# Keys and queries of an attention kernel from one product, the queries sent through DRAM

## The chip, the cores and the metric

The kernel runs on one NeuronCore of a Trainium2 chip. The metric is device time in microseconds (us), as the median of several runs. Everything is computed in float32.

## The reference, cut to what matters

There are 8 images of 192 channels and 64 x 64 = 4096 positions. Layer 0 is an attention over the positions with 24 channels in query and key; layer 1 is an elementwise chain (a small network of its own for each channel), called the density here.

```python
# layer 0
g = gn(x)                                     # 32 groups, mean 0 and variance 1
q = prelu(conv1x1(g, w1, b1), a1)             # 24 channels
k = prelu(conv1x1(g, w2, b2), a2)             # 24 channels
v = prelu(conv1x1(g, wa, ba), aa)             # 192 channels
score = softmax(einsum('bnc,bcm->bnm', q, k), axis=2)
x = x + einsum('bnm,bmc->bnc', score, v)
# layer 1
g = gn(x)
lower, upper = cumulative(g - 0.5), cumulative(g + 0.5)   # 4 layers 1-3-3-3-1: softplus, tanh
sign = -sign(lower + upper)
x = x + maximum(abs(sigmoid(sign * upper) - sigmoid(sign * lower)), 1e-6)
```

## The kernel before, in words

Channels lie on partitions, three to a row (g of 3), so that 64 partitions hold the 192 channels. The lower 64 partitions hold the first half of the positions and the upper 64 the second half. A **piece** (d, 8 an image) is 256 positions of each half, loaded from x into one of four buffers xi (192 KB for each half); a **chunk** (c, 4 an image) is two pieces.

The stream is a loop of 8 images x 128 **steps**, written out in order by hand. An image has 8 blocks n of 512 query positions, and 16 steps a block. In each step TensorE computes two score products (L769, tile sc) for the next step and two products for a later block's row maxima (L697, tile mx), ScalarE takes the exponential of the scores (L773), and TensorE multiplies the exponentials with the values (L784). VectorE reduces mx to row maxima (L705). The score and maximum products contract over only 24 channels (25 with the maximum's row), so the keys and the queries are kept in all four groups of 32 partitions, and the products of a step use different groups. sc and mx have one PSUM buffer each. The maxima run 22 steps ahead of the scores (LEAD).

What else has to be done goes in between. A scheduler (`job`, `start_job`) starts at most one **job** in a step, which takes a free PSUM bank pair, one of two pairs of scratch tiles (pra, prb), and a few TensorE products; its evaluation on ScalarE and VectorE comes one and two steps later. Jobs are the keys, the queries and the values of a piece, the transposes of the maxima (L734) and of the output (L817), the group norm's averages, and the folding of the norm into the weights (L523 to L555). A keys job is three products over 128 rows (L601), the weights of both halves placed block by block; a queries job is six products over 64 rows, three for each half (L630), whose weights repeat the query channels in the four groups. `prelu` (L583 to L589) evaluates both: two activations with Relu on ScalarE (L585), and one combination on VectorE (L588), whose output is kt for keys and the chunk's tile q for queries.

The keys and values of the next image are made during this one (`prepare`, at steps 30 and later), and its first queries at step 97. The queries of chunk c are made in the 32 steps before their first use (`within`). For each use a piece of x is loaded anew: 28 loads of a piece per image, in kinds of their own ("st" for statistics, "k" and "kv" for keys and values, "q", "v").

The density of image b (L994 to L1026, some 276 VectorE operations of 128 x 1024) is worked off during image b + 1 by credits. In each step VectorE gets a rate that is the work left, divided by the steps left; a job with TensorE time pe and VectorE time cost changes the credit as follows, so that more density work stands beside a longer step:

```python
            credit["DVE"] += pe - cost
            credit["ACT"] += pe - act
...
            rate = left * COST["DVE"] / max(1, (units[0].key[0] + 2) * IMG + 15 - t) + OTHER
```

Some of the density's last part runs on GpSimd. Loads and stores are issued by SyncE in the order of the steps. A head of about 94 us prepares image 0, whose pieces have buffers of their own ("first"), and a tail of about 370 us ends the density of image 7, partly on TensorE (L967).

Of the kernel before, what the change touches and what calls it, by code (L numbers as in the profile page):

```python
# [17 lines left out]
def kernel(  # L18
# [39 lines left out]

    nc = tc.nc
# [26 lines left out]
    small = ctx.enter_context(tc.tile_pool(name="small", bufs=2))  # L86
    dens = ctx.enter_context(tc.tile_pool(name="dens", bufs=1))
# [24 lines left out]
    for i in range(4):  # L112
        t = xin.tile([128, 3, P], F32, tag=f"xi{i}", name=f"xi{i}")
        spare.append(t)
    free = {"xi": 4, "xc": 3}
# [34 lines left out]
    w1r = const.tile([128, 3, 128], F32, name="w1r")  # L150
    w2r = const.tile([128, 3, 128], F32, name="w2r")
    wa_sb = const.tile([128, 3, C], F32, name="wa_sb")
    bq = const.tile([128, 2], F32, name="bq")
    bk = const.tile([128, 2], F32, name="bk")
    ba_row = const.tile([128, C], F32, name="ba_row")
    one_row = const.tile([128, 128], F32, name="one_row")
    slope = const.tile([128, 3], F32, name="slope")
    nslope = const.tile([128, 3], F32, name="nslope")
    for t in (bq, w1r, w2r, ba_row, one_row):
        nc.vector.memset(t, 0.0)  # L160
# [3 lines left out]
    nc.vector.tensor_reduce(out=bk[:, 0:1], in_=ident[:, CR::32], axis=AX.X, op=ALU.add)  # L164
# [11 lines left out]
    for k in range(4):  # L176
        nc.scalar.dma_start(out=bq[32 * k : 32 * k + CR, 0:1], in_=b1.unsqueeze(1))
        nc.scalar.dma_start(out=bk[32 * k : 32 * k + CR, 0:1], in_=b2.unsqueeze(1))
    for i, a in enumerate((a1, a2, aa)):
        nc.scalar.dma_start(out=slope[:, i : i + 1], in_=a.partition_broadcast(128))  # L180

    def spread():

        for k in range(4):
            at = slice(32 * k, 32 * k + CR)
            nc.gpsimd.tensor_copy(w1r[:, :, at], s1)

            p = slice(R * (k % 2), R * (k % 2) + R)
            nc.gpsimd.tensor_copy(w2r[p, :, at], s2[p])
        for g in range(3):  # L190
            nc.gpsimd.tensor_copy(
                wa_sb[:, g, :].rearrange("p (h r) -> p h r", h=3),
                sa[:, g, :].rearrange("p (r h) -> p h r", h=3),
            )
        for s in range(2):
            p = slice(R * s, R * s + 1)
            nc.gpsimd.tensor_copy(
                ba_row[p].rearrange("p (h r) -> p h r", h=3),
                sb[p].rearrange("p (r h) -> p h r", h=3),
            )  # L200

    def negatives():
        for t in (bq, bk):
            nc.vector.tensor_scalar(t[:, 1:2], t[:, 0:1], -1.0, None, ALU.mult)
        nc.vector.tensor_scalar(nslope, slope, -1.0, None, ALU.mult)
# [128 lines left out]
    for k, cols in (("a", F), ("b", 2 * C)):  # L334
        pair = []
        for i in range(2):
            u = work.tile([128, cols], F32, tag=f"pr{k}{i}", name=f"pr{k}{i}")
            pair.append(u)
        scratch.append(pair)
# [58 lines left out]
    def work_off(t, rate):  # L398
        now[0] = t
        run_due(t)  # L400
        start_job(t)
        run_due(t)
        held = set()
        for kind, fn in list(loads):
            if kind == "xi":

                room = free["xi"] - max(0, 2 - sum(k[0] in "qv" for k in xi))
            else:
                room = free["xc" if kind == "xc" else "xi"]
            if room > 0 and kind not in held:  # L410
# [103 lines left out]
    def weights(b, then):  # L514
# [3 lines left out]
        def scale():  # L518
            for k, src, n in (("q", w1r, 2), ("k", w2r, 1), ("v", wa_sb, 1)):
                d = wf[k, b] = fold.tile(  # L520
                    [128, 3, src.shape[2]], F32, tag=f"w{k}", bufs=n, name=f"w{k}_{b}"
                )
                nc.scalar.activation(d, src, AF.Copy, scale=res[:, 1:2])  # L523
            mb = cell["mb"] = fold.tile([128, 128], F32, tag="mb", name=f"mb_{b}")
            nc.vector.tensor_copy(mb, res[:, 0:1].to_broadcast([128, 128]))

        def products():
            pf = cell["pf"]
            p = slice(0, R)
            for g in range(3):  # L530
                cell["write"](nc.tensor.matmul(
                    pf[:, 0:2], lhsT=wf["q", b][p, g, :], rhs=res[p, 0:2],
                    start=g == 0, stop=g == 2,
                ))
            for g in range(3):
                cell["write"](nc.tensor.matmul(
                    pf[:, 2:4], lhsT=wf["k", b][:, g, :], rhs=res[:, 0:2],
                    start=g == 0, stop=g == 2,
                ))
            for g in range(3):  # L540
                cell["write"](nc.tensor.matmul(
                    pf[:, 4 : 4 + C], lhsT=cell["mb"][p], rhs=wf["v", b][p, g, :],
                    start=g == 0, stop=g == 2,
                ))

        def offsets():
            pf = cell["pf"]
            for k, src, at_, n in (("bq", bq, 0, 2), ("bk", bk, 2, 1)):
                d = wf[k, b] = fold.tile([128, 2], F32, tag=k, bufs=n, name=f"{k}_{b}")
                cell["read"](nc.vector.tensor_tensor(  # L550
                    d[:, 0:1], src[:, 0:1], pf[:, at_ : at_ + 1], ALU.subtract
                ))
                nc.vector.tensor_scalar(d[:, 1:2], d[:, 0:1], -1.0, None, ALU.mult)
# [38 lines left out]

    def keys(b, d, what, done):
        t = xi[what, b, d]

        def make(pk, u):
# [3 lines left out]
            for g in range(3):  # L600
                write(nc.tensor.matmul(  # L601
                    pk[:, 0:P], lhsT=wf["k", b][:, g, :], rhs=t[:, g, :],
# [3 lines left out]
            c, h = divmod(d, 2)  # L606
            p = slice(64 * (c % 2), 64 * (c % 2) + 64)
            at_ = (c // 2) * F + h * P
            first, last = prelu(
                ("k", b, d), kt[b][p, at_ : at_ + P], pk[p, 0:P], wf["bk", b][p], nslope[p, 1:2],  # L610
                [x[p, 0:P] for x in u], read,
            )
            return [
                (0, lambda: None, 0.0, 0.0, 1.3), (1, first, 0.0, 0.9, 0.0),
                (2, last, 0.45, 0.0, 0.0),
# [4 lines left out]
    def queries(b, d, what, done):  # L620
        t = xi[what, b, d]
        c, h = divmod(d, 2)

        def make(pq, u):
            if (b, c) not in qt:
                qt[b, c] = work.tile([128, 2, F], F32, tag="q", bufs=2, name=f"q_{b}_{c}")
            for g in range(3):
                for s in range(2):
                    p = slice(R * s, R * s + R)
                    nc.tensor.matmul(  # L630
                        pq[:, s, 0:P], lhsT=wf["q", b][p, g, :], rhs=t[p, g, :],
                        start=g == 0, stop=g == 2,
                    )
            done()
            first, last = prelu(
                ("q", b, d), qt[b, c][:, :, h * P : h * P + P], pq[:, :, 0:P], wf["bq", b], nslope[:, 0:1],
                [x[:, 0:F].rearrange("p (s n) -> p s n", s=2) for x in u],
            )
            return [
                (0, lambda: None, 0.0, 0.0, 1.4), (1, first, 0.0, 1.4, 0.0),  # L640
                (2, last, 0.75, 0.0, 0.0),
            ]

        job(make, h, 0.5 if d == 2 else 2, 2, F)
# [46 lines left out]
    def max_products(b, n, j, k, sc):  # L691
        assert all(i in made for i in (("q", b, n), ("k", b, 2 * k), ("k", b, 2 * k + 1)))
# [539 lines left out]
    def use(b, d, what, t, k, q, v, after=0):  # L1232

        left = [k + q + 2 * v]
# [6 lines left out]
        def begin():  # L1241
            if what != "first":
                visit(b, d, what)
            at(max(now[0] + 4, after), work)

        def work():
            if q:
                queries(b, d, what, done)
# [6 lines left out]
        if what == "first":  # L1255
            at(t, work)
        else:
            at(t, lambda: request("q" if what in "qv" else "xi", begin))

    def prepare(b, t):  # L1260
# [7 lines left out]
        def normed():  # L1268
            for i, c in enumerate(ORDER):
                for h in range(2):  # L1270
                    what = "kv" if i < 2 else "k"
                    use(b, 2 * c + h, what, max(now[0], t + 30 + 6 * (2 * i + h)), 1, 0, i < 2)

            for h in range(2):
                use(b, h, "q", t + 92, 0, 1, 0, t + 97)
# [4 lines left out]
        for i in (2, 3):  # L1280
            for h in range(2):
                use(b, 2 * ORDER[i] + h, "v", t + 100 + 4 * i + 2 * h, 0, 0, 1, t + 107 + 4 * i)
        for h in range(2):
            use(b, 2 + h, "q", t + 122, 0, 1, 0, t + IMG)

    def within(b, t):
        for d in range(4 if b else 2, NP):
            at_ = t + 32 * (d // 2 - 1)
            use(b, d, "q" if b else "first", at_ - 6 if b else at_, 0, 1, 0, at_)
# [31 lines left out]
    todo = [(queries, 0), (keys, 0), (queries, 1)] + [(keys, d) for d in range(1, NP)]  # L1321
# [6 lines left out]
    while todo or ahead:  # L1328
# [10 lines left out]
        if (0, 3, 3) in [i for _, i in pair]:  # L1339
            max_end(0, 0)  # L1340
        go_on()
# [72 lines left out]
```

## Time and profile before

| | |
|---|---|
| median of 3 runs | 4918.28 us (4916.8 to 4919.44) |
| time of the profiled execution | 4916.79 us |
| its span | 4915.0 us |
| mean granted TensorE clock | 0.987 |
| first scores / last step's scores start | 94.05 / 4545.37 us |

The span runs from the first to the last instruction of the profiled execution; its time has 1.8 us more around it. In a group row of the profile, the columns after "x" and the count are the busy time of the whole group in us and the mean of one instruction in ns, then the engine's idle time before these instructions, with what ended it. A float32 product shows as two MATMUL rows.

### The profile page before, as it was taken

To read this page: it belongs to the slowest core of one execution; us is meant where nothing else is said; L and a number is where in the kernel's file an instruction comes from. 1 tells how busy PE (TensorE), PEld (TensorE's weight loads), DVE (VectorE), ACT (ScalarE), POOL (GpSimd) and SP (SyncE) were. 2 spreads that over 40 slices of the span, in tenths; PEclk is the share of its full clock that TensorE was granted. 3 is DMA by queue.
4 is the path that set the end of the run, shared out by engine and by line. 5 is a ranking of instruction groups with operands and counts; after the bars stand their busy time and mean duration, and the time that the engine had idled before them with its cause. 6 is when DMAs were issued, how large, how long until landed. Compare 5 with 4: busy or idle time off the path is not lost.

```text
span 4915.0 us, 69887 instructions
## 1 busy us (share of the span) xinstructions
PE 4740.1 (96%) x29152; PEld 3505.3 (71%) x29152; DVE 4312.6 (88%) x4442; ACT 3194.5 (65%) x3709; POOL 514.0 (10%) x506
## 2 busy tenths in 40 slices
PE   7999999999999999999999999999999999999496
PEld 5777777777777777777777777777777777777232
DVE  5433359999999999999999999999999999998987
ACT  2333347776767766776776767776767767676765
POOL 0000001111011110210111200111111111111000
PEclk9999999999999999999999999999999999999798
DMA  2000020111200111010110111011111101000000
GB/s 56 26 22 18 14 52 4 32 28 31 51 18 18 42 37 34 23 37 24 42 30 21 32 40 40 18 31 32 31 34 32 28 22 28 11 22 5 9 13 13
DMA packets 111953, 135.49 MB, mean 28 GB/s; under 512 B 14738, under 2 KB 93076, under 8 KB 111636
## 3 DMA queue, kind: packets, MB, share of 16 engines
q1 hardware_dynamic: 110432, 130.65, 10.9%
q8 instruction: 228, 3.74, 0.3%
q14 instruction: 89, 0.73, 0.1%
q10 hardware_dynamic: 1204, 0.37, 0.0%
HBM read 105.82 MB, written 25.17 MB: 27 GB/s over the span
## 4 chain that ended last, share of the span: by engine, by line
PE 78%; DVE 16%; ACT 4%; issue 1%; POOL 1%; DMA 0%; ACTq 0%; SPq 0%; DVEq 0%; POOLq 0%
PE b L784 46%; PE sc L769 18%; DVE d L1026 10%; DVE rm L705 4%; PE b L658 4%; PE b L967 2%; PE b L630 2%; PE b L601 1%; PE sc_tail L967 1%; PE mx_tail L967 1%; PE mx L697 1%; PE b L817 1%; ACT d L1019 1%; ACT d L1009 1%; ACT e L773 1%
## 5 line engine op out<-in xcount | busy, mean ns | idle before, releaser
L784 PEld LDWEIGHTS b<-v,e 128*128 128x128 f32 x16384 | 2655.1, 190 | 777.0 <-issue 772.5
L784 PE MATMUL b<-v,e 128*128 128x193 f32 x16384 | 2958.9, 334 | 0.0
L773 ACT ACTIVATE e<-sc 128x1024 f32<-128x1024 f32 x1024 | 1046.7, 1022 | 1456.3 <-PE mx L697 1414.0
L705 DVE TENSOR_REDUCE rm<-mx 128x1 f32<-128x1024 f32 x1002 | 1223.3, 1221 | 459.6 <-PE mx L697 454.2
L769 PE MATMUL sc<-q,k 25*128 25x512 f32 x4096 | 1155.2, 640 | 16.8 <-ACT e L773 16.4
L697 PE MATMUL mx<-k,q 24*128 24x512 f32 x4008 | 1130.4, 640 | 4.9 <-DVE rm L705 4.9
L1026 DVE SCALAR_TENSOR_TENSOR d<-d,wsp,d 128x1024 f32<-128x1024 f32 x768 | 988.0, 1288 | 44.3 <-ACT d L1019 33.6
L1026 DVE SCALAR_TENSOR_TENSOR d<-d,lc,d 128x1024 f32<-128x1024 f32 x765 | 981.6, 1291 | 18.1 <-ACT d L1003 5.1
L1026 DVE SCALAR_TENSOR_TENSOR d<-d,tf,d 128x1024 f32<-128x1024 f32 x543 | 683.9, 1280 | 3.5 <-ACT d L1009 3.4
L1009 ACT ACTIVATE d<-d 128x1024 f32<-128x1024 f32 x543 | 569.6, 1055 | 57.1 <-DVE d L1026 55.7
L769 PEld LDWEIGHTS sc<-q,k 25*128 25x128 f32 x4096 | 306.2, 182 | 250.2 <-issue 195.8
L1114 POOL MEMSET pause<- 128x1 f32 x240 | 23.7, 99 | 3965.9 <-DVE d L1026 3965.9
L1019 ACT ACTIVATE d<-d,cb,wsp 128x1024 f32<-128x1024 f32 x351 | 433.3, 1235 | 0.8 <-DVE d L1026 0.2
L994 ACT ACTIVATE d<-xc,bn,wn 128x1024 f32<-128x1024 f32 x288 | 354.1, 1236 | 2.8 <-DVE bn L491 2.0
L1003 ACT ACTIVATE d<-xc,bn,wn 128x1024 f32<-128x1024 f32 x255 | 315.7, 1238 | 0.0
L697 PEld LDWEIGHTS mx<-k,q 24*128 24x128 f32 x4008 | 299.6, 182 | 16.9 <-DVE rm L705 13.5
L1149 POOL TENSOR_TENSOR d<-d,d 128x512 f32<-128x512 f32 x80 | 169.5, 2119 | 0.2
L1161 POOL TENSOR_TENSOR d<-d,d 128x512 f32<-128x512 f32 x80 | 167.7, 2097 | 0.0
L1169 POOL TENSOR_TENSOR d<-d,d 128x512 f32<-128x512 f32 x80 | 156.4, 1955 | 2.3 <-POOL pause L1114 0.6
L658 PE MATMUL b<-wv,xi 64*128 64x192 f32 x1344 | 139.5, 340 | 1.4 <-ACT pra L585 1.4
L658 PEld LDWEIGHTS b<-wv,xi 64*128 64x128 f32 x1344 | 106.5, 186 | 26.9 <-issue 20.9
L967 PE MATMUL b<-d,v 128*128 128x512 f32 x204 | 95.2, 618 | 17.0 <-ACT d L994 17.0
(171 smaller groups left out, 2373.5 us busy)
## 6 DMA issues: line engine op xcount, KB each, us to landing
xi<-in_x_dram SPq DMA_DIRECT2D x392, 192.0 KB, 3.4
xc<-in_x_dram SPq DMA_DIRECT2D x64, 384.0 KB, 8.0
out_dram<-xc SPq DMA_DIRECT2D x96, 256.0 KB, 3.2
d<-in_x_dram SPq DMA_DIRECT2D x16, 192.0 KB, 4.0
d<-in_wat_dram ACTq DMA_DIRECT2D x2, 144.0 KB
cb<-in_den_b_dram SPq DMA_DIRECT2D x6, 2.2 KB, 2.1
ff<-in_den_f_dram SPq DMA_DIRECT2D x6, 2.2 KB, 2.2
bq<-in_b_dram ACTq DMA_DIRECT2D x4, 0.1 KB
```

Of the source, the lines that this page charges most:

```text
L658: nc.tensor.matmul(pv[:, s, 0:C], lhsT=t[p, g, k * 128 : k * 128 + 128] if g < 3 else one_row[p], rhs=wf["v", b][p, g, :] if g < 3 else wf ...
L697: nc.tensor.matmul(sc[:, s, :], lhsT=tile_of(qt[b, n // 2], n, j)[r], rhs=kt[b][r, u : u + F], start=True, stop=True,)
L705: nc.vector.tensor_reduce(out=rowmax[b, n][:, j, k : k + 1], in_=sc, axis=AX.XY, op=ALU.max)
L769: nc.tensor.matmul(sc[:, s, :], lhsT=kt[b][r, k : k + 128], rhs=qt[b, n // 2][r, :, u : u + 256], start=True, stop=True,)
L773: return lambda: nc.scalar.activation(e, sc, AF.Exp)
L784: nc.tensor.matmul(a[:, j, 0 : C + 1], lhsT=e[:, s, j * 128 : j * 128 + 128], rhs=v[:, s, p % 4, :], start=p == 0 and s == 0 and j % 2 == ...
L967: nc.tensor.matmul(out[:, h, :], lhsT=diag[g][:, 3 * i + n - 1 if n else 9 + i, :], rhs=src[:, h * F : h * F + F], start=n == 0, stop=n == 3,)
L994: nc.scalar.activation(self.buf[k], self.src(), AF.Tanh, bias=bn[:, s, g, 0, i : i + 1], scale=wn[:, g, 0, i : i + 1],)
L1003: nc.scalar.activation(self.buf[k], self.src(), AF.Identity, bias=bn[:, s, g, 1, i : i + 1], scale=wn[:, g, 1, i : i + 1],)
L1009: nc.scalar.activation(self.buf[k], self.buf["l", k[1], k[2]], AF.Tanh)
L1019: nc.scalar.activation(self.buf[k], self.buf["l", n - 1, 0], AF.Identity, bias=offset, scale=wsp[:, g, w : w + 1],)
L1026: nc.vector.scalar_tensor_tensor(dst, src, factor, dst, ALU.mult, ALU.add)
```

## The change

The weights of keys and queries are placed side by side in two tiles `wr`, one for the even and one for the odd chunks. Three products over 128 rows now give both, keys in one half of the 128 output partitions and queries in the other. One evaluation writes them into a tile `kq` of 128 x 256 (three buffers). From there two DMAs of SyncE bring the keys into kt and the queries into a DRAM tile `qd`. `queries(b, c)` then loads a chunk's queries from DRAM four times, once into each group of 32 partitions. There are three buffers xi instead of four, the loads of x for queries are gone, all loads of pieces stand in one line, and both pairs of scratch tiles are 384 columns wide.

```diff
-    for i in range(4):
+    for i in range(3):
         t = xin.tile([128, 3, P], F32, tag=f"xi{i}", name=f"xi{i}")
         spare.append(t)
-    free = {"xi": 4, "xc": 3}
+    free = {"xi": 3, "xc": 3}
...
-        for k in range(4):
-            at = slice(32 * k, 32 * k + CR)
-            nc.gpsimd.tensor_copy(w1r[:, :, at], s1)
-
-            p = slice(R * (k % 2), R * (k % 2) + R)
-            nc.gpsimd.tensor_copy(w2r[p, :, at], s2[p])
+        for i in range(2):
+            for k in range(4):
+                at = slice(32 * k, 32 * k + CR)
+                p = slice(R * (k % 2), R * (k % 2) + R)
+                nc.gpsimd.tensor_copy(wr[i][p, :, at], (s2 if k // 2 == i else s1)[p])
...
-    for k, cols in (("a", F), ("b", 2 * C)):
+    for k in "ab":
         pair = []
         for i in range(2):
-            u = work.tile([128, cols], F32, tag=f"pr{k}{i}", name=f"pr{k}{i}")
+            u = work.tile([128, 2 * C], F32, tag=f"pr{k}{i}", name=f"pr{k}{i}")
...
+    qd = []
+    for i in range(2):
+        t = dram.tile([NC, 64, F], F32, tag=f"qd{i}", name=f"qd{i}")
+        qd.append(t)
+
     def keys(b, d, what, done):
         t = xi[what, b, d]
+        c, h = divmod(d, 2)
+        i = c % 2
...
                 write(nc.tensor.matmul(
-                    pk[:, 0:P], lhsT=wf["k", b][:, g, :], rhs=t[:, g, :],
+                    pk[:, 0:P], lhsT=wf[i, b][:, g, :], rhs=t[:, g, :],
                     start=g == 0, stop=g == 2,
                 ))
             done()
-            c, h = divmod(d, 2)
-            p = slice(64 * (c % 2), 64 * (c % 2) + 64)
-            at_ = (c // 2) * F + h * P
+            kq = work.tile([128, P], F32, tag="kq", bufs=3, name=f"kq_{b}_{d}")
             first, last = prelu(
-                ("k", b, d), kt[b][p, at_ : at_ + P], pk[p, 0:P], wf["bk", b][p], nslope[p, 1:2],
-                [x[p, 0:P] for x in u], read,
+                None, kq, pk[:, 0:P], wf["b", i, b], nslope[:, i : i + 1],
+                [x[:, 0:P] for x in u], read,
             )
+
+            def move():
+                last()
+                k, q = (slice(64 * j, 64 * j + 64) for j in (i, 1 - i))
+                u = (c // 2) * F + h * P
+                nc.sync.dma_start(out=kt[b][k, u : u + P], in_=kq[k])
+                nc.sync.dma_start(out=qd[b % 2][c, :, h * P : h * P + P], in_=kq[q])
+                at(now[0] + 1, lambda: made.update((("k", b, d), ("qd", b, d))))
+
             return [
                 (0, lambda: None, 0.0, 0.0, 1.3), (1, first, 0.0, 0.9, 0.0),
-                (2, last, 0.45, 0.0, 0.0),
+                (2, move, 0.45, 0.0, 0.0),
             ]
...
-    def queries(b, d, what, done):
-        t = xi[what, b, d]
-        c, h = divmod(d, 2)
-        def make(pq, u):
-            if (b, c) not in qt:
-                qt[b, c] = work.tile([128, 2, F], F32, tag="q", bufs=2, name=f"q_{b}_{c}")
-            for g in range(3):
-                for s in range(2):
-                    p = slice(R * s, R * s + R)
-                    nc.tensor.matmul(
-                        pq[:, s, 0:P], lhsT=wf["q", b][p, g, :], rhs=t[p, g, :],
-                        start=g == 0, stop=g == 2,
-                    )
...
-        job(make, h, 0.5 if d == 2 else 2, 2, F)
+    def queries(b, c):
+        assert all(("qd", b, 2 * c + h) in made for h in range(2))
+        q = qt[b, c] = work.tile([128, 2, F], F32, tag="q", bufs=2, name=f"q_{b}_{c}")
+        for k in range(4):
+            nc.sync.dma_start(
+                out=q[32 * k : 32 * k + 32],
+                in_=qd[b % 2][c].rearrange("(s r) n -> r s n", s=2),
+            )
+        made.add(("q", b, c))
...
-            for h in range(2):
-                use(b, h, "q", t + 92, 0, 1, 0, t + 97)
+            at(t + 97, lambda: queries(b, 0))
...
-        for h in range(2):
-            use(b, 2 + h, "q", t + 122, 0, 1, 0, t + IMG)
...
-        for d in range(4 if b else 2, NP):
-            at_ = t + 32 * (d // 2 - 1)
-            use(b, d, "q" if b else "first", at_ - 6 if b else at_, 0, 1, 0, at_)
+        for c in range(1, NC):
+            at(t + 32 * (c - 1) + 1, lambda c=c: queries(b, c))
...
-    todo = [(queries, 0), (keys, 0), (queries, 1)] + [(keys, d) for d in range(1, NP)]
+    todo = [(keys, d) for d in range(NP)]
...
+        if ("qd", 0, 1) in made and (0, 0) not in qt:
+            queries(0, 0)
```

More of the change, by code (lines that the diff above doesn't have):

```diff
@@ L86 @@
     small = ctx.enter_context(tc.tile_pool(name="small", bufs=2))
+    dram = ctx.enter_context(
+        tc.tile_pool(name="dram", bufs=1, space=bass.MemoryType.DRAM)
+    )
     dens = ctx.enter_context(tc.tile_pool(name="dens", bufs=1))
@@ L148 @@
             nc.vector.tensor_copy(gq[:, s, :, i], gs)
-    w1r = const.tile([128, 3, 128], F32, name="w1r")
-    w2r = const.tile([128, 3, 128], F32, name="w2r")
+    wr = []
+    bb = []
+    slope = []
+    for i in range(2):
+        w = const.tile([128, 3, 128], F32, name=f"wr{i}")
+        wr.append(w)
+        w = const.tile([128, 1], F32, name=f"bb{i}")
+        bb.append(w)
+        w = const.tile([128, 1], F32, name=f"slope{i}")
+        slope.append(w)
     wa_sb = const.tile([128, 3, C], F32, name="wa_sb")
-    bq = const.tile([128, 2], F32, name="bq")
-    bk = const.tile([128, 2], F32, name="bk")
     ba_row = const.tile([128, C], F32, name="ba_row")
     one_row = const.tile([128, 128], F32, name="one_row")
-    slope = const.tile([128, 3], F32, name="slope")
+    vslope = const.tile([128, 1], F32, name="vslope")
     nslope = const.tile([128, 3], F32, name="nslope")
-    for t in (bq, w1r, w2r, ba_row, one_row):
+    for t in (*wr, ba_row, one_row):
         nc.vector.memset(t, 0.0)
@@ L162 @@
     nc.vector.memset(one_row[R : R + 1], 1.0)
-    nc.vector.tensor_reduce(out=bk[:, 0:1], in_=ident[:, CR::32], axis=AX.X, op=ALU.add)
+    for i in range(2):
+        nc.vector.tensor_reduce(
+            out=bb[i], in_=ident[:, 64 * i + CR : 64 * i + 64 : 32], axis=AX.X, op=ALU.add
+        )
     st = bufs[0]
@@ L175 @@
         nc.scalar.dma_start(out=sb[R * s : R * s + 1], in_=ba.unsqueeze(0))
-    for k in range(4):
[L177 to L180, printed above, removed]
-    def spread():
-        for k in range(4):
-            at = slice(32 * k, 32 * k + CR)
-            nc.gpsimd.tensor_copy(w1r[:, :, at], s1)
-            p = slice(R * (k % 2), R * (k % 2) + R)
-            nc.gpsimd.tensor_copy(w2r[p, :, at], s2[p])
+    for i in range(2):
+        for k in range(4):
+            b_ = b2 if k // 2 == i else b1
+            nc.scalar.dma_start(out=bb[i][32 * k : 32 * k + CR], in_=b_.unsqueeze(1))
+        for k in range(2):
+            a = a2 if k == i else a1
+            nc.scalar.dma_start(
+                out=slope[i][64 * k : 64 * k + 64], in_=a.partition_broadcast(64)
+            )
+    nc.scalar.dma_start(out=vslope, in_=aa.partition_broadcast(128))
+    def spread():
+        for i in range(2):
+            for k in range(4):
+                at = slice(32 * k, 32 * k + CR)
+                p = slice(R * (k % 2), R * (k % 2) + R)
+                nc.gpsimd.tensor_copy(wr[i][p, :, at], (s2 if k // 2 == i else s1)[p])
         for g in range(3):
@@ L202, in negatives @@
     def negatives():
-        for t in (bq, bk):
-            nc.vector.tensor_scalar(t[:, 1:2], t[:, 0:1], -1.0, None, ALU.mult)
-        nc.vector.tensor_scalar(nslope, slope, -1.0, None, ALU.mult)
+        for i, a in enumerate((*slope, vslope)):
+            nc.vector.tensor_scalar(nslope[:, i : i + 1], a, -1.0, None, ALU.mult)
     negmax = const.tile([128, 4, 128], F32, name="negmax")
@@ L404, in work_off @@
         for kind, fn in list(loads):
[L405 to L410, printed above, removed]
+            if free[kind] > 0 and kind not in held:
                 loads.remove((kind, fn))
@@ L518, in scale @@
         def scale():
-            for k, src, n in (("q", w1r, 2), ("k", w2r, 1), ("v", wa_sb, 1)):
+            for k, src in ((0, wr[0]), (1, wr[1]), ("v", wa_sb)):
                 d = wf[k, b] = fold.tile(
-                    [128, 3, src.shape[2]], F32, tag=f"w{k}", bufs=n, name=f"w{k}_{b}"
+                    [128, 3, src.shape[2]], F32, tag=f"w{k}", name=f"w{k}_{b}"
                 )
@@ L529, in products @@
             p = slice(0, R)
-            for g in range(3):
-                cell["write"](nc.tensor.matmul(
-                    pf[:, 0:2], lhsT=wf["q", b][p, g, :], rhs=res[p, 0:2],
-                    start=g == 0, stop=g == 2,
[L534 to L539, printed above, removed]
+            for i in range(2):
+                for g in range(3):
+                    cell["write"](nc.tensor.matmul(
+                        pf[:, 2 * i : 2 * i + 2], lhsT=wf[i, b][:, g, :], rhs=res[:, 0:2],
+                        start=g == 0, stop=g == 2,
+                    ))
             for g in range(3):
@@ L547, in offsets @@
             pf = cell["pf"]
-            for k, src, at_, n in (("bq", bq, 0, 2), ("bk", bk, 2, 1)):
-                d = wf[k, b] = fold.tile([128, 2], F32, tag=k, bufs=n, name=f"{k}_{b}")
+            for i in range(2):
+                d = wf["b", i, b] = fold.tile([128, 2], F32, tag=f"b{i}", name=f"b{i}_{b}")
                 cell["read"](nc.vector.tensor_tensor(
-                    d[:, 0:1], src[:, 0:1], pf[:, at_ : at_ + 1], ALU.subtract
+                    d[:, 0:1], bb[i], pf[:, 2 * i : 2 * i + 1], ALU.subtract
                 ))
@@ L591, in prelu @@
         return first, last
+    qd = []
+    for i in range(2):
+        t = dram.tile([NC, 64, F], F32, tag=f"qd{i}", name=f"qd{i}")
+        qd.append(t)
     def keys(b, d, what, done):
         t = xi[what, b, d]
+        c, h = divmod(d, 2)
+        i = c % 2
         def make(pk, u):
@@ L616, in make @@
             ]
         job(make, d % 2, cols=P)
-    def queries(b, d, what, done):
-        t = xi[what, b, d]
-        c, h = divmod(d, 2)
-        def make(pq, u):
-            if (b, c) not in qt:
-                qt[b, c] = work.tile([128, 2, F], F32, tag="q", bufs=2, name=f"q_{b}_{c}")
-            for g in range(3):
-                for s in range(2):
-                    p = slice(R * s, R * s + R)
-                    nc.tensor.matmul(
-                        pq[:, s, 0:P], lhsT=wf["q", b][p, g, :], rhs=t[p, g, :],
-                        start=g == 0, stop=g == 2,
-                    )
[L634 to L637, printed above, removed]
-            )
[L639 to L642, printed above, removed]
-        job(make, h, 0.5 if d == 2 else 2, 2, F)
+    def queries(b, c):
+        assert all(("qd", b, 2 * c + h) in made for h in range(2))
+        q = qt[b, c] = work.tile([128, 2, F], F32, tag="q", bufs=2, name=f"q_{b}_{c}")
+        for k in range(4):
+            nc.sync.dma_start(
+                out=q[32 * k : 32 * k + 32],
+                in_=qd[b % 2][c].rearrange("(s r) n -> r s n", s=2),
+            )
+        made.add(("q", b, c))
@@ L691, in max_products @@
     def max_products(b, n, j, k, sc):
-        assert all(i in made for i in (("q", b, n), ("k", b, 2 * k), ("k", b, 2 * k + 1)))
+        assert all(i in made for i in (("q", b, n // 2), ("k", b, 2 * k), ("k", b, 2 * k + 1)))
         for s in range(2):
@@ L1230, in look, with use @@
         at(t, lambda: request("xi", begin))
-    def use(b, d, what, t, k, q, v, after=0):
-        left = [k + q + 2 * v]
+    def use(b, d, what, t, k, v, after=0):
+        left = [k + 2 * v]
         def done():
@@ L1241, in begin @@
         def begin():
-            if what != "first":
-                visit(b, d, what)
+            visit(b, d, what)
             at(max(now[0] + 4, after), work)
         def work():
-            if q:
-                queries(b, d, what, done)
             if k:
@@ L1253, in work @@
                     values(b, d, i, what, done)
[L1255 to L1258, printed above, removed]
+        at(t, lambda: request("xi", begin))
     def prepare(b, t):
@@ L1271, in normed @@
                     what = "kv" if i < 2 else "k"
-                    use(b, 2 * c + h, what, max(now[0], t + 30 + 6 * (2 * i + h)), 1, 0, i < 2)
-            for h in range(2):
-                use(b, h, "q", t + 92, 0, 1, 0, t + 97)
+                    use(b, 2 * c + h, what, max(now[0], t + 30 + 6 * (2 * i + h)), 1, i < 2)
+            at(t + 97, lambda: queries(b, 0))
         for d in range(NP):
@@ L1281, in prepare @@
             for h in range(2):
-                use(b, 2 * ORDER[i] + h, "v", t + 100 + 4 * i + 2 * h, 0, 0, 1, t + 107 + 4 * i)
-        for h in range(2):
-            use(b, 2 + h, "q", t + 122, 0, 1, 0, t + IMG)
+                use(b, 2 * ORDER[i] + h, "v", t + 100 + 4 * i + 2 * h, 0, 1, t + 107 + 4 * i)
     def within(b, t):
-        for d in range(4 if b else 2, NP):
-            at_ = t + 32 * (d // 2 - 1)
-            use(b, d, "q" if b else "first", at_ - 6 if b else at_, 0, 1, 0, at_)
+        for c in range(1, NC):
+            at(t + 32 * (c - 1) + 1, lambda c=c: queries(b, c))
         for c in range(2):
```

## The prediction

> **What bounds the kernel now.** I read the page's busy times and chain first, then the chain and the busy times of single 16-step stretches, then the timeline for the length of one step, and last the groups that the change touches.
>
> ```profile
> span 4915.0 us, 69887 instructions
> PE 4740.1 (96%) x29152; PEld 3505.3 (71%) x29152; DVE 4312.6 (88%) x4442; ACT 3194.5 (65%) x3709; POOL 514.0 (10%) x506
> ...
> PE 78%; DVE 16%; ACT 4%; issue 1%; POOL 1%; DMA 0%; ACTq 0%; SPq 0%; DVEq 0%; POOLq 0%
> ```
>
> The chain runs on TensorE for 78% of the span and on VectorE for 16%; no DMA is in it. The mean hides the middle, so here are the busy times of two stretches of one image (length; PE, PEld, DVE, ACT, POOL; granted clock, DMA share, GB/s), and the chain of the first by line:
>
> ```profile
> 2057.63:2129.41 71.78, 71.78 (x463) 54.39 (x462) 69.86 (x68) 51.94 (x61) 8.76 (x8) 1.00 0.09 25
> 2129.41:2195.65 66.24, 66.12 (x407) 49.95 (x406) 65.08 (x62) 50.70 (x57) 13.76 (x12) 1.00 0.24 50
> ...
> by line: PE b L784 47.2%; PE sc L769 18.9%; DVE d L1026 15.7%; DVE rm L705 6.4%; PE b L658 4.2%; PE b L630 4.2%; PE b L817 0.9%; DVE q L740 0.8%; DVE v L588 0.7%; DVE k L588 0.7%; PE mx L697 0.6%; issue 0.2%
> ```
>
> TensorE is busy without a gap, VectorE 97 to 98%. The query products (L630) stand in the chain with 4.2% of 71.78 us = 3.0 us, the whole of the two that run there. The timeline gives their price: from one step's scores to the next,
>
> ```profile
> 1428.76 0.70 PE L769 MATMUL sc<-q,k 25*128 25x512 f32 x2
> ...
> 1432.64 0.70 PE L769 MATMUL sc<-q,k 25*128 25x512 f32 x2
> ...
> 2092.34 0.70 PE L769 MATMUL sc<-q,k 25*128 25x512 f32 x2
> ...
> 2096.22 1.57 PE L630 MATMUL b<-xi,wq 64*128 64x256 f32 x12
> 2097.71 0.70 PE L769 MATMUL sc<-q,k 25*128 25x512 f32 x2
> ```
>
> A step without a job takes 3.88 us, one with a query job 2097.71 - 2092.34 = 5.37. Read so over the whole stream, steps with a key job take 5.18 and with a value job 5.38, almost all at these same lengths: TensorE sets the step. Scores run from 94.05 to 4545.37; image 0 takes 555 us, images 1 to 6 take 560 to 566.
>
> ```profile
> L630 PE MATMUL b<-xi,wq 64*128 64x256 f32 x672 | 87.7, 393 | 0.0
> L601 PE MATMUL b<-xi,wk 128*128 128x256 f32 x336 | 81.8, 379 | 0.1
> L585 ACT ACTIVATE pra<-b,bq 128x512 f32<-128x512 f32 x126 | 79.4, 686 | 0.7 <-PE b L630 0.7
> L588 DVE SCALAR_TENSOR_TENSOR q<-pra,nslope,pra 128x512 f32<-128x512 f32 x64 | 52.6, 822 | 4.5 <-ACT pra L585 4.5
> L588 DVE SCALAR_TENSOR_TENSOR k<-prb,nslope,prb 64x256 f32<-64x256 f32 x47 | 23.4, 498 | 2.5 <-ACT prb L585 2.1
> ```
>
> **The change part by part.** *Query jobs go.* Sixty-two run in the stream (six for image 0, eight for each of the seven others) and two before it. Each costs 5.37 - 3.88 = 1.50 us of TensorE, all of it on the path: 62 x 1.50 = 93 us. ScalarE loses two activations of 686 ns a job and VectorE one operation of 0.74 us (the median of L588's q); these ran beside TensorE and shorten nothing by themselves.
>
> *The joint product.* The key product already streams 256 columns through 128 rows with 128 weight columns, of which 64 are then thrown away. The new weights have the same shape, so a key step stays at 5.18 us. Its two activations and its VectorE operation go from 64 to 128 partitions of 256 elements. No row has that form; rows of 128 x 384 and 128 x 512 cost ScalarE 490 and 686 ns against 462 for 64 x 256, so time follows the elements of a partition: between zero (same columns) and, if it doubled, 0.9 us on ScalarE and 0.5 on VectorE. I take zero. The folded weights and offsets of an image (L523 to L555) keep their number; a product of 64 rows (264 ns) becomes one of 128 (267 ns).
>
> *The round trip.* A piece gets two moves of 64 KB (keys into kt, queries to DRAM), a chunk four loads of 128 KB: 32 DMAs an image, against 16 loads of x of 192 KB that go; 3.1 MB against 3.1 MB. SyncE takes 1.18 us for two issues, so 32 take 19 us of 560, against 9 that go. A move waits on SyncE for the piece's VectorE operation, and later loads of x and stores of the output stand behind it. It stands in its own step, though, and x is loaded four steps (15.5 us) ahead of its use. VectorE has to find one of three kq buffers free, so it waits for moves three pieces back, at least two steps ago. The trace has no such DMA; the nearest row is the load of x:
>
> ```profile
> xi<-in_x_dram SPq DMA_DIRECT2D x392, 192.0 KB, 3.4
> ```
>
> Four issues (2.4 us) and 3.4 us to landing make some 6 us; the loads are issued nine steps, at least 35 us, ahead of the first maximum product that reads them, and the queries have been written some 50 steps earlier. Beside that row a rule of the Trainium skill speaks against the change: "DMA: Bandwidth & Descriptors", section "Anatomy of one DMA", gives each transfer about 2 us that do not shrink with its size, and its section "Bandwidth" wants transfers of 1 MiB and calls those under 64 KB dominated by descriptors. By its fit (given for GpSimd's path, so an estimate here) 64 and 128 KB take 2.15 and 2.3 us, 16 of each 71 us an image; were these paid in line, the kernel would lose 570 us and the sum would turn over. By the trace DMA has 0% of the chain although a 192 KB load takes 3.4 us, because it starts steps ahead. I take zero for the stream and keep a few us a chunk as the upper end. If the 35 us of cover were gone, each chunk would cost its 6 us, 31 x 6 = 186 us.
>
> *Three x buffers for four.* Twenty pieces an image are loaded instead of 28, and the scheduler hands out a buffer only after the product that frees it. Zero; at most a job comes some steps later.
>
> *The density's order.* Query jobs gave VectorE slack: 1.50 - 0.74 = 0.76 us each. The scheduler credits VectorE 1.4 us and charges 0.75 for each; without it the same density work is spread evenly, 8 x 0.65 = 5.2 us an image over 128 steps, also into stretches that are at 98 to 99% already. An image of VectorE work goes from 547.5 us (the sum of eight stretches) to 541.5, TensorE's image from about 563 to 551: VectorE would be at 98.3% instead of 97.2%. The maximum product (L697) has one PSUM buffer, so a late reduction (L705) stops TensorE. Stretches that are at 99% today are at most 1.4 us longer than TensorE needs, most under 0.5. With half a us more in most of eight stretches I give back 3 us an image for images 1 to 6, and 5 of the 9 us of the last image, where the chain is more VectorE than TensorE: 18 + 5 = 23.
>
> *The head.* First products now need queries that have been to DRAM: keys of piece 1 are evaluated at about 40 us, two moves issue to 41.2, land at 43.5; four loads to 46, landing near 49, and the move of piece 3 stands behind them on SyncE. The first maximum product starts at 46.9 now, so 2 us are lost. Two fewer jobs shorten the end of the head by two value-only rounds of 1.4 us. Net -1, between -4 and +4. The tail after 4546 us is untouched: zero.
>
> Sum against the profiled execution's 4916.8 us: -93 + 23 - 1 = -71, so 4846. The median of the runs shown is 1.5 us above it, so 4847.
>
> **Rivals.** *VectorE becomes the bound.* For it: the 16% in the chain, 97 to 98% busy, the single buffer of mx. Then images 1 to 7 gain only what VectorE loses, 0.74 us for each of the 54 query jobs in their steps, 40 us, while image 0, with no density beside it, keeps its 8 x 1.5 = 12: 52 us in all, 4866. Against it: 10 us of VectorE an image stay idle at the new length. *No give-back.* The 99% stretches show that the schedule can be that tight: 93 + 3, 4822. *Late queries.* Here the kernel gets slower: L697 waits at the first step of each chunk for the loads, with everything behind it on TensorE. It takes over when the loads land 71/31 = 2.3 us past the 35 us, that is, when SyncE's queue is held for some 30 us. For it: SyncE is in order and has waits of up to 119.6 us (for a product that frees an x buffer). Against it: those are waits in program order, which end at the step in which the load stands. At 5 us late a chunk: 4846 + 155 = 5001. *The joint product is not free*: with key evaluation doubled, 64 x 0.5 us on a full VectorE, 32 us come back, 4879; if waits for kq buffers cost VectorE another 39/64 = 0.6 us a piece, no change remains.
>
> **How the numbers follow.** Likeliest 0.53 (4834 to 4858 on its own); VectorE-bound 0.22 (4858 to 4875); no give-back 0.14 (4818 to 4834); costs that eat it all, within 0.2%, 0.04; late queries 0.07. The range 4827 to 4872 leaves out late queries, the tie and the ends of two cases. 0.2% is about 10 us, what a measurement of this kernel can tell from no change: faster 0.89, same 0.04, slower 0.07.
>
> **What would show it.** Right: no L630-like group; key steps still 5.18 us; empty steps mostly at 3.88 with some longer ones, VectorE over 98% in the middle; image 0 at about 543 us and images 1 to 6 at 553 to 555; no row in which PE waits for a DMA after the head. Wrong: PE mx waiting for q's load; kq operations of VectorE waiting for DMA; key steps above 5.3; images above 558.

## The result, and the profile after

The changed kernel takes 4848.81 us (median of 4 runs, 4845.56 to 4850.88) against 4918.86 before (the three runs of the table ahead of the prediction and a fourth): a ratio of 0.9858, 95% interval 0.9844 to 0.9872. It is 70 us faster; 71 were forecast for the profiled executions. The page of its profiled execution (4845.56 us, the fastest of its four):

```profile
span 4843.8 us, 68352 instructions
PE 4656.6 (96%) x28384; PEld 3443.8 (71%) x28384; DVE 4260.6 (88%) x4378; ACT 3116.6 (64%) x3581; POOL 523.3 (11%) x506
...
PE 79%; DVE 14%; ACT 4%; issue 1%; POOL 1%; DMA 0%; ACTq 0%; DVEq 0%; POOLq 0%
...
xi<-in_x_dram SPq DMA_DIRECT2D x280, 192.0 KB, 3.4
...
q<-qd SPq DMA_DIRECT2D x128, 128.0 KB, 2.6
k<-kq SPq DMA_DIRECT2D x64, 64.0 KB, 1.9
qd<-kq SPq DMA_DIRECT2D x64, 64.0 KB, 2.1
```

TensorE has 84 us less to do. The new transfers land in 1.9 to 2.6 us, and DMA still has 0% of the chain. The groups of the changed lines, by form (after the bar: busy us of the group, mean ns of one, then idle time before):

```profile
L620 PE MATMUL b<-xi,w 128*128 128x256 f32 x336 | 81.7, 379 | 0.0
...
L596 ACT ACTIVATE prb<-b,b 128x256 f32<-128x256 f32 x100 | 41.6, 472 | 0.5 <-PE b L620 0.5
...
L599 DVE SCALAR_TENSOR_TENSOR kq<-prb,nslope,prb 128x256 f32<-128x256 f32 x53 | 25.2, 476 | 4.0 <-ACT prb L596 4.0
```

The joint product costs what the key product did (81.8 us, 379 ns), and twice the partitions cost its evaluation next to nothing (462 and 498 ns before). No group like the query products is left.

Read from the start of each step's scores, image by image:

| part | before, us | after, us | difference | forecast |
|---|---|---|---|---|
| head (to the first scores) | 94.05 | 88.88 | -5.2 | -1 |
| image 0 | 555.3 | 543.1 | -12.2 | -12 |
| images 1 to 6 together | 3380.4 | 3329.8 | -50.6 | -54 |
| image 7 to its last step | 515.6 | 511.3 | -4.3 | -4 |
| tail | 369.6 | 370.8 | +1.2 | 0 |
| span | 4915.0 | 4843.8 | -71.2 | -71 |

Images 1 to 6 gain 8.4 us each instead of 12. Where the rest went is seen when the steps of an image are set against the shortest step with the same job (3.88 us for none, 5.18 keys, 5.38 values and so on). What lies above that in images 2 to 6, in us an image (a step is counted by the start of its scores):

| steps | before | after |
|---|---|---|
| 0 to 12 | 0.0 | 0.0 to 0.1 |
| 13 to 17 | 3.1 to 4.8 | 9.3 to 11.4 |
| 18 to 33 | 1.2 to 2.9 | 1.1 to 2.9 |
| 34 to 127 | 2.3 to 4.9 | 0.6 to 3.2 |

The growth is in one place, and most of it in one step: of the 9.3 to 11.4 us step 17 has 5.5 to 7.2 (1.9 to 3.6 before). These are the steps 16 and 17 of image 4 in the timeline of the changed kernel (start, duration in us, engine, line), and then two stretches of it with the granted TensorE clock in the third column from the right:

```profile
2361.96 3.66 DVE L1037 SCALAR_TENSOR_TENSOR d<-d,tf,d 128x1024 f32<-128x1024 f32 x3
...
2365.53 2.67 DVE L1037 SCALAR_TENSOR_TENSOR d<-d,lc,d 128x1024 f32<-128x1024 f32 x2
...
2368.12 1.22 DVE L716 TENSOR_REDUCE rm<-mx 128x1 f32<-128x1024 f32 x1
```

```profile
2361.63 1.13 PE L708 MATMUL mx<-k,q 24*128 24x512 f32 x4
...
2365.50 1.13 PE L780 MATMUL sc<-q,k 25*128 25x512 f32 x4
2369.39 1.77 PE L708 MATMUL mx<-k,q 24*128 24x512 f32 x4 [2.77 <-DVE rm L716]
2371.09 5.51 PE L795 MATMUL b<-v,e 128*128 128x193 f32 x16
2376.53 0.70 PE L780 MATMUL sc<-q,k 25*128 25x512 f32 x2
```

```profile
2365.50:2371.00 5.50, 2.73 (x9) 0.59 (x8) 5.39 (x7) 2.26 (x4) 0.00 (x0) 0.89 0.01 3
2371.00:2376.53 5.53, 5.53 (x18) 5.01 (x16) 4.84 (x5) 1.05 (x1) 0.00 (x0) 0.50 0.00 0
```

VectorE does five density operations before the reduction at 2368.12, which is due when the maximum products that start at 2361.63 are done. TensorE can't start the next maximum product, because mx has one buffer, and stands for 2.77 us. Then the value products take 5.51 us instead of 2.88: the granted clock is 0.50 through the rest of the step. A step of 3.88 us lasts 11.03.

The same stall stands in step 17 of all five images, but the slow clock after it has two lengths. Here is the whole step, first of image 4 and then of image 5:

```profile
2365.50:2376.53 11.03, 8.26 (x25) 5.60 (x24) 10.23 (x11) 3.31 (x4) 0.00 (x0) 0.69 0.00 1
2921.58:2930.99 9.41, 6.64 (x26) 4.47 (x25) 9.27 (x11) 3.31 (x4) 0.00 (x0) 0.82 0.00 1
```

A mean clock of 0.69 over 11.03 us is half clock for 6.8 us, and 0.82 over 9.41 us is half clock for 3.4. Images 2 and 6 are like image 5 (9.40 and 9.44 us), image 3 is like image 4 (10.96). The difference of 1.6 us is the price of 3.4 us at half clock. By that estimate the slow clock has 3.3 of the 7.15 us in images 3 and 4 and 1.7 of the 5.5 us in the others, and the stall, with the products that no longer overlap, has 3.8 in each.

The schedule itself, as the code works it out, says why so much density work stands there. An image's density is due by step 15 of the image after the next, and the rate is the work left divided by the steps left. If the work is late, the rate runs away:

```
rate (us a step) and, in brackets, density operations placed, steps 10 to 14, images 2 to 6
before   3.0-3.3 (2-3)   3.15 (2)   3.35 (2)   3.76 (2)   4.98 (3)
after    3.3-3.5 (2-3)   3.46 (2)   3.76 (1)   4.98 (3)   6.20 (5)
```

### The profile page after: what moved, and what is told of

Same layout as the page of the kernel before. It is cut to its first block, busy times and chain, and to the rows that moved or that the text cites. A ratio compares the mean times of both kernels' runs of the same rounds, so it can differ in the third digit from the quotient of the medians.

```text
span 4843.8 us, 68352 instructions
## 1 busy us (share of the span) xinstructions
PE 4656.6 (96%) x28384; PEld 3443.8 (71%) x28384; DVE 4260.6 (88%) x4378; ACT 3116.6 (64%) x3581; POOL 523.3 (11%) x506
## 4 chain that ended last, share of the span: by engine, by line
PE 79%; DVE 14%; ACT 4%; issue 1%; POOL 1%; DMA 0%; ACTq 0%; DVEq 0%; POOLq 0%
PE b L795 48%; PE sc L780 18%; DVE d L1037 9%; PE b L669 4%; DVE rm L716 3%; PE b L978 2%; PE b L620 1%; PE sc_tail L978 1%; PE mx_tail L978 1%; PE b L828 1%; ACT e L784 1%; PE mx L708 1%; ACT d L1005 1%; ACT d L1030 1%; ACT d L1020 1%
## 5 line engine op out<-in xcount | busy, mean ns | idle before, releaser
L1005 ACT ACTIVATE d<-xc,bn,wn 128x1024 f32<-128x1024 f32 x288 | 353.6, 1234 | 12.2 <-DVE bn L506 11.4
```

The lines of the kernel that those rows point to most:

```text
L1005: nc.scalar.activation(self.buf[k], self.src(), AF.Tanh, bias=bn[:, s, g, 0, i : i + 1], scale=wn[:, g, 0, i : i + 1],)
```

## The experiments

**Only TensorE's part back.** The old jobs' six products, 62 times, on constant operands; 62 jobs, no evaluation.

```diff
+            for g in range(3):
+                for s in range(2):
+                    p = slice(R * s, R * s + R)
+                    nc.tensor.matmul(
+                        pq[:, s, 0:P], lhsT=wr[0][p, g, :], rhs=kt[b][p, 0:P],
+                        start=g == 0, stop=g == 2,
+                    )
+            return [(0, lambda: None, 0.0, 0.0, 1.4)]
```

> The changed kernel with the old query jobs' six products put back as jobs (62 of them, at their old steps, with constant weights and keys as data, their result unused; no evaluation, no load of x). Theory A, that TensorE's time is what was gained and VectorE's lateness in a few steps gives some of it back: 62 x 1.50 = 93 us come back, less the some 25 us of give-back, since VectorE gets its slack again: 4905 to 4920 us, image 0 back at 555, steps with such a job 5.38. Theory B, that VectorE was and is the bound and the gain came from its fewer operations: less than 45 us come back, below 4893. Theory C, that the gain came from fewer loads and a shorter head: under 20 us.

Measured: 4915.48 us (12 runs), a ratio of 0.9996 to before, 95% interval 0.9988 to 1.0005. Image 0 takes 555.1 us again and images 2 to 6 563 to 564; the steps with such a job take 5.38. The returned products, as the trace has them:

```profile
L663 PE MATMUL b<-k,wr x744: 376/376/480, 109.5 to 4322.0; 64*128 64x256 f32 x186
```

They are the old ones to the nanosecond (376 in the middle). With TensorE's time back the whole gain is gone, so fewer loads and fewer VectorE operations are worth nothing while the products are there. (The jobs bring back their places in the scheduler and their 1.4 us of credit as well; that the products themselves are the time is read from the steps of 5.38 us.) The 67 us that came back are less than 93 mainly because steps 13 to 17 got calmer again (5.5 to 7.0 us for 9.3 to 11.4). They are not as calm as before the change: this schedule, too, reaches a rate of 6.20 at step 14 and puts four or five operations there. In images 2 to 6 TensorE then stands for some 3.7 us once, in step 15, and waits for an exponential, which stands behind density operations on ScalarE (read in image 4).

**Only VectorE's part back.** One operation of the old size at each old place; the scheduler is not told.

```diff
+            at(t0 + 2, lambda: ghost2(b))
...
+        nc.vector.scalar_tensor_tensor(gu[0], kt[b][:, 0:F], nslope[:, 0:1], kt[b][:, 0:F], ALU.mult, ALU.add)
```

> The changed kernel with one more VectorE operation of 128 x 512 for each old query job in the stream (62, at the steps of the old ones; it combines a tile of keys, its output is unused; nothing else moves, the scheduler is not told). Theory A: VectorE at 98% has little room, so images 1 to 7 lose part of 54 x 0.74 = 40 us, image 0 nothing: 10 to 30 us, 4859 to 4879. Theory B (VectorE is the bound everywhere): the full 40 us or more, 4889 and up. Theory D (TensorE alone is the bound): within 5 us of the changed kernel.

Measured: 4867.7 us, 19 more than the changed kernel (ratio to before 0.9899, 0.9883 to 0.9916). The tile's rows:

```profile
L664 DVE SCALAR_TENSOR_TENSOR gu<-k,nslope x62: 734/742/744, 127.2 to 4281.5; 128x512 f32<-128x512 f32 x62
```

Image 0 stays at 543.1. Of the 40 us put into images 1 to 7, about half lengthen the run: VectorE is close behind TensorE, not ahead of it. Both "TensorE alone" and "VectorE everywhere" fall. Beside the run above this means that the two parts work together: without the products, the VectorE operations that went with them are worth some 19 of the 70 us.

**The density's rate capped.** One line in `density_step`, in the changed kernel (3.0 and 2.8) and in the kernel before (3.0).

```diff
             rate = left * COST["DVE"] / max(1, (units[0].key[0] + 2) * IMG + 15 - t) + OTHER
+            rate = min(rate, 3.0)
```

> The changed kernel with the density's rate capped at 3.0 us a step; uncapped it rises to 6.2 at step 14 of an image, where an image's last density work falls due, and puts five operations between two reductions. Theory A1, that the give-back sits in that burst and in the slow TensorE clock after it: steps 13 to 17 fall from 10 us over their shortest lengths to 3 or less in images 2 to 6, others unchanged: 25 to 45 us less, 4805 to 4825. Theory A2, that VectorE at 98% is late anyway: the excess moves to other steps, 4840 to 4852.

> The kernel before with the density's rate capped at 3.0 us a step; uncapped it reaches 5.0 there and puts three operations into step 14. Theory A1 (the burst grew with the change, so that most of the cap's 28 us belongs to the changed kernel): steps 13 to 17 of images 2 to 6 stand at 3 to 5 us over their shortest and may lose 2 of them: 5 to 12 us less, 4905 to 4912. Rival (the cap helps either kernel alike): 28 us less, 4889. If A1 holds, the change alone is worth some 88 us with the burst out of the way in both.

> The changed kernel with the density's rate capped at 2.8 us a step, just above the mean that is needed. Theory A1: as good as 3.0 in steps 13 to 17, a little less work done before an image's last steps; 4815 to 4826. If a tighter cap only shifts lateness to VectorE's later steps: 4826 to 4845.

Measured: 4820.93 us with 3.0 (ratio to before 0.9800, 0.9786 to 0.9815) and 4811.4 with 2.8 (0.9784, 0.9769 to 0.9799): 28 and 37 us less than the changed kernel. In the kernel before, 3.0 gives 4912.91 us (0.9992, 0.9985 to 0.9999): 4 us less, a little under what was expected; 2.8 came out 4 us below its range. In steps 13 to 17 of images 2 to 6 the changed kernel has 0.8 to 2.7 us left with 3.0 and 0 to 0.5 with 2.8, the kernel before 0.4 to 0.8. The other steps do not stay as they were: up to 5 us an image come back there in each of the three runs. The waits of TensorE for the reduction over the whole run, of the kernel before, of the changed kernel, and of the changed kernel with 3.0 (us in all, times, longest):

```profile
PEld mx L697 <- DVE rm L705: 13.5, 14, 1.7
PE mx L697 <- DVE rm L705: 4.9, 7, 0.8
```

```profile
PEld mx L708 <- DVE rm L716: 29.1, 22, 3.6
PE mx L708 <- DVE rm L716: 13.8, 5, 2.8
```

```profile
PEld mx L708 <- DVE rm L716: 3.5, 7, 0.9
```

The five stalls of 2.8 us in the PE row, one in each of images 2 to 6, are gone with 3.0. Without the cap the rate of images 2 to 6 is over 3.0 in steps 8 to 14 alone (10 to 14 in the kernel before), so the cap acts on the burst and its run-up: they were the give-back of images 1 to 6. With 3.0 in both kernels the change is worth 4912.9 - 4820.9 = 92 us, beside 62 x 1.50 = 93 us of TensorE. That nothing is given back holds for the sum only. By the profiled executions images 1 to 6 gain 78.5 us, 6.5 more than their 48 jobs account for (why stays open), and image 7 gains 4.0 of its 9, as it did without the cap. The cap at 2.8 is the fastest version that was run. Its chain:

```profile
span 4805.7 us, 68347 instructions
...
PE 70%; DVE 23%; ACT 4%; issue 2%; POOL 1%; DMA 1%; SPq 0%; ACTq 0%; DVEq 0%; POOLq 0%
```

VectorE's share rises from 14 to 23%. No run separates the burst's wait from the slow clock after it; the estimate from step 17 above is all there is.

**Query loads late.** One step ahead instead of nine.

```diff
-            at(t + 97, lambda: queries(b, 0))
+            at(t + 105, lambda: queries(b, 0))
...
-            at(t + 32 * (c - 1) + 1, lambda c=c: queries(b, c))
+            at(t + 32 * (c - 1) + 9, lambda c=c: queries(b, c))
```

> The changed kernel with the query loads of a chunk issued one step before the first maximum product that reads them instead of nine. Theory A (the round trip is hidden with room to spare; four issues and the landing take some 4.5 us against a step of 3.9): at most 31 chunks x 2 us = 60 us more, and less where SyncE runs ahead of the step: 4850 to 4910, with the rows of PE mx waiting for a DMA to show it. Rival (the round trip costs TensorE something today already): a full 4.5 us a chunk on top, 4985 and up.

Measured: 4870.56 us, 22 more than the changed kernel (ratio to before 0.9902, 0.9887 to 0.9917). Now TensorE waits for the round trip. Waits of the profiled execution (4876.27 us, the slowest of the four), then the landing of the loads:

```profile
PEld mx L708 <- issue: 8.6, 6, 2.6
...
PE mx L708 <- DMA q<-qd: 5.9, 6, 1.8
...
PEld mx L708 <- DMA q<-qd: 2.0, 9, 0.3
```

```profile
DMA to landing us min/median/max: 2.4/3.2/9.5
```

The changed kernel has no row in which TensorE waits for a DMA. The step most hit is the first of the last chunk's maxima, up to 9.92 us for 4.32; part of this is the slow clock again (in image 3 the value products of that step take 4.56 us for 2.88). Two moves and two loads of x stand ahead of the query loads on SyncE there (image 3). For most other chunks the loads were issued a step or more ahead of their use and cost nothing. The cover was real and is ample: taking away eight of nine steps costs half a per cent.

**Query loads twice.** Eight loads a chunk for four.

```diff
-        for k in range(4):
+        for k in (0, 1, 2, 3, 0, 1, 2, 3):
```

> The changed kernel with every chunk's four query loads issued twice, the second four after the first have landed (64 DMAs of 128 KB more an image than before the change's own 32). Theory A (the round trip is covered by nine steps): no change, within 5 us of the changed kernel. Rival (SyncE's queue or the transfers are near a limit): some us a chunk, 30 us or more on top.

Measured: 4849.91 us (0.9861, 0.9847 to 0.9876), 1 us from the changed kernel. With twice the query loads neither SyncE's queue nor the transfers reach a limit. (The doubled loads add 16 an image, not 64; the expectation counted wrongly.)

**Four xi buffers, two kq.**

```diff
-    for i in range(3):
+    for i in range(4):
...
-            kq = work.tile([128, P], F32, tag="kq", bufs=3, name=f"kq_{b}_{d}")
+            kq = work.tile([128, P], F32, tag="kq", bufs=2, name=f"kq_{b}_{d}")
```

> The changed kernel with four buffers xi again and two buffers kq for three (memory does not hold both). Theory A (neither number matters): within 6 us of the changed kernel. Rival (three xi buffers hold jobs back): 10 us or more less. Rival (VectorE waits for moves with two kq buffers): more, with waits of kq operations for DMAs.

Measured: 4845.67 us (0.9855, 0.9840 to 0.9869), 3 us less, which is within the spread of the runs. The run changes both numbers at once, so a small gain from the fourth xi buffer could hide a small loss from the third kq buffer. The waits of the kq operations on VectorE show that two buffers are one too few only four times, for 6.5 us of VectorE in all:

```profile
  DMA qd<-kq: 6.5, 4
```

## Why the prediction was right or wrong, point by point

- *Query jobs, 62 x 1.50 = 93 us of TensorE:* right. Putting the products back gives the time of before, and with the burst out of both kernels the difference is 92 us.
- *The joint product is free:* right; key steps stay at 5.18 us, and the evaluation goes by the elements of a partition (472 and 476 ns for 128 x 256, 462 and 498 for 64 x 256). The three ScalarE rows that I drew this from were thin support: 462, 490 and 686 ns for 256, 384 and 512 elements do not lie on a line.
- *The round trip is hidden:* right. Loads land in 2.6 us, not 3.4, TensorE never waits for them after the head, and doubling them costs 1 us. The estimate from the fit of the Trainium skill ("DMA: Bandwidth & Descriptors", section "Anatomy of one DMA") was 2.15 and 2.3 us for 64 and 128 KB; the medians here, 1.9 and 2.1 for the moves and 2.6 for the loads, are near it. The rule of its section "Bandwidth" against small transfers doesn't decide here, since the price is paid steps ahead; the price begins to show when the cover shrinks to one step (22 us).
- *Three xi buffers:* right as far as the run shows; a fourth, with one kq buffer fewer, gives 3 us.
- *The give-back of 23 us:* the size is nearly right, the mechanism in part wrong. Images 1 to 6 give back 72 - 50.6 = 21.4 us for 18 and image 7 4.7 for 5, 26 in all. I saw that VectorE's slack goes and that mx has one buffer, and I spread half a microsecond over most stretches. The trace shows the steps from 34 on below their old excess, and all of the growth in steps 13 to 17, where the schedule's due time makes the rate run away and the clock is halved after the stall. Nothing in the forecast's reading asked when work falls due; the rate's formula, quoted ahead of the forecast, held the answer. That the size came out all the same is luck: half a microsecond a stretch and one step of 9.4 to 11 us have little to do with each other. VectorE's share did not go over 98% as forecast, because the image stayed longer by the stall; image 3 took 556.4 us for the 553 to 555 forecast, and VectorE 541.08 of them, 97.2%:

```profile
sum 556.44, PE 551.88 PEld 417.38 DVE 541.08 ACT 392.44 POOL 78.08; mean PE 68.98 PEld 52.17 DVE 67.64 ACT 49.06 POOL 9.76
```

- *The head, -1 us:* the sign is right, the size too small. The first maximum product starts at 44.17 us instead of 46.9, where I had it 2 us later: the keys of piece 1 are evaluated at 37.4 us, not at about 40, and four loads issue in 1.79 us, not 2.4, and land sooner. Executions of the same head start their first scores between 88.6 and 93.4 us. The four with three kq buffers and no slow clock before the first scores start them at 88.6 to 89.0, and the kernel before did at 92.2 and 94.05 in two, so the gain is 3 to 5 us.
- *The sum, -71:* that it met the profiled executions' 71.2 to a fraction of a microsecond is luck. The head took 4 us more than forecast, and the give-back of 26 us and a tail 1.2 us longer took these away again.
- *Rivals:* VectorE as the bound (4866) and no give-back (4822) did not come true for the change as it was made. That one more VectorE operation a job gives 4867.7 us is a coincidence with the first: were VectorE the bound, those operations would have cost their full 40 us, and they cost 19. The second is reached only with the cap (4820.9). Late queries never came up.

## What to carry to other kernels

In this kernel work taken off the engine that binds was gained in full only where the next engine's work stood evenly; look for the steps in which a planner's due time, not the mean load, puts several operations ahead of one that the first engine waits for. When a change takes work out of a static schedule, its rates and credits are worth setting again: here one `min` gave another 28 to 37 us. A round trip through DRAM cost nothing here with its issue nine steps ahead of its use, and moving it later is a quick way to see how much cover it has.

## What the hardware showed that was not expected

- A TensorE stall of 2.8 us was followed by 3.4 or 6.8 us at a granted clock of 0.50 (value products of up to 5.51 us for 2.88). The Trainium skill's "TensorE: Matmul & The Clock Gate", section "HAM oscillation", describes such a fall after gaps longer than some 3.4 us; the trace has the last products before the gap ending near 2366.6, so the gap is 2.8 us on TensorE and 3.6 us on its weight loads.
- The length of a stall alone did not decide whether the clock fell. In the kernel before, step 17 of images 2 and 3 has the same stall of less than 1 us, far under those 3.4; the value products after it ran at a mean clock of 0.62 in image 2 and of 1.00 in image 3:

```profile
1282.48 1.13 PE L697 MATMUL mx<-k,q 24*128 24x512 f32 x4 [0.84 <-DVE rm L705]
1283.54 4.56 PE L784 MATMUL b<-v,e 128*128 128x193 f32 x16
...
1847.24 1.13 PE L697 MATMUL mx<-k,q 24*128 24x512 f32 x4 [0.85 <-DVE rm L705]
1848.30 2.88 PE L784 MATMUL b<-v,e 128*128 128x193 f32 x16
```

- An issue on SyncE took 0.43 us for a query load of 128 KB (median) and 0.52 and 0.60 for the two moves of 64 KB.
- The head's length differs by up to 5 us between executions; in the profiled one with the cap at 2.8, the mean clock between 75 and 95 us was 0.85, in the changed kernel's 0.95 (and there the slow stretch came after the first scores).
